# A four-bit quantization that starts two blocks earlier, and one more block in seven products

## The chip, the cores and the metric

The kernel runs on one core of a Trainium2 chip. A core has TensorE (PE, with the weight loads PEld), VectorE (DVE), ScalarE (ACT), GpSimd (POOL) and SyncE (SP), which here only issues transfers. Each engine works through its own queue in order, and semaphores make one wait for another. The metric is the device time of one execution in microseconds, the median of three runs. The profile is of one execution.

## The reference

128 matrices x of 64x512 are each multiplied by a 64x64 matrix that is picked from a table by an index. The result goes through two linear layers whose weights are made ternary (three values and a common factor), with an exact GELU between them. The output y of the second layer is quantized to four bits with one scale for the whole tensor, which comes from the largest |y|, and x is added.

```python
w = weights[conditions]
c = jnp.einsum('bct,bcd->bdt', x, w)
h = jax.nn.gelu(ternary_linear(c, W1, b1), approximate=False)   # 512 -> 2048
y = ternary_linear(h, W2, b2)                                   # 2048 -> 512
scale = jnp.max(jnp.abs(y)) / 7 + 1e-8
out = x + jnp.clip(jnp.round(y / scale), -7, 7) * scale
```

## The kernel before

The work goes through 16 blocks (`NB`), n = 0 to 15, of eight matrices each. A block has four pairs of matrices (`PAIRS`), 512 columns in all. Of each block the kernel first makes the mixed input (`condition` or `condition7`: `mix` on PE, then a high and a low part of the result by ACT and DVE), then goes through the 2048 hidden values in 16 steps of 128 (`hc` = 0 to 15), and adds each step's share of the second layer up in four accumulators (`py`). `result` turns these into y, `largest` takes the largest |y| of each row, and `keep` stores y to DRAM. The mixed input of block n + 1 is made during block n: `fetch` gathers the table's rows (POOL issues an indirect transfer into `wg`), `place` puts them into the matrix `diag`, and `mix` multiplies.

There are two ways through a block. `eight(s)` does one step: eight matmuls of 512 columns for the first layer (`ph`), and the second layer's matmuls two steps behind. `pair(n, k)` does two steps at once, k = 0 to 7, with `seven`: of the four products of a two-by-two split it computes seven smaller ones instead of eight, with sums of the weights (`sums`), in PSUM tiles x, y and z of 256 columns. ACT and DVE put the products together (`ha`, `hb`), ACT applies GELU and takes the high part, and DVE the low part (`low`). `behind(i)` is called at seven places of `seven` and issues what else belongs there: POOL's widened weights (`widen7`, `widen2`, into `wf`), the gather and placing of the next block, its mixing in pairs 3 to 6, the results of the block before in pairs 0 and 1, and its largest values in pairs 1 and 2. Blocks 2 to 13 go by `pair` (`SEVEN`), blocks 0, 1, 14 and 15 by `eight`.

The scale is speculative. `KNOWN` is 14: after block 13 the largest value of blocks 0 to 13 is found (`widened` reduces `ymax` to one column and copies it into all columns of `ones_f`, `largest_of` transposes this on PE and reduces again, `steps_of` makes `scale` and `inverse`). With it the output is made, while blocks 14 and 15 are still being computed, in 30 half blocks (`units`, in the order of blocks 2 to 13, 0, 1, 14): `quantize` on ACT, `add_x` on DVE one unit behind, `store` on SP, and `ahead_x`, which loads x two blocks ahead (`fetch_x`, and for blocks 0 and 1 also y from DRAM, `y_back`). `advance` does one such unit. The y of blocks 2 and up stays in SBUF until then, in the pool `big` of 20 buffers. At the end the largest value of the blocks left out is compared with the known one, and only if it is larger everything is quantized again under `tc.If`.

The queues are in program order on every engine (`InOrder`), so the place of a call in the text is its place in the queues of all the engines that it uses. Buffers come from pools, and who takes one waits until the readers of its former tile are through.

Of the kernel before, what the change touches and what calls it, by code (L numbers as in the profile page):

```python
# [8 lines left out]
F32 = mybir.dt.float32  # L9
# [11 lines left out]
P = 128  # L21
# [18 lines left out]
def tile_cond_ternary_ffn(  # L40
# [15 lines left out]
    B, C, T = x.shape  # L56
    S, _, D = weights.shape
    NT = T // P
    NH = W1.shape[1]
# [5 lines left out]
    GH = NH // NG  # L65
    WCH = GH * T
    LAG = 2
    SEVEN = range(2, 14)
    KNOWN = NB - 2
    AWAY = 2  # L70
    HALF = BLK // 2
    ADDED = [3, 4, 5, 6, 7, 12, 13, 14]
# [17 lines left out]
    def pair_of_pairs(h):  # L90
        return slice(h * PAIRS // 2, (h + 1) * PAIRS // 2)

    def load_x(n):

        xt = big.tile([P, PAIRS, T], F32, tag="big", name=f"xt_{n}")
        for h in range(2):
            js = pair_of_pairs(h)
            sp.dma_start(out=xt[:, js, :], in_=x_blk[n][:, js, :])
        return [xt[:, pair_of_pairs(h), :] for h in range(2)]

    def half_x(n, h):

        xt = half.tile([P, PAIRS // 2, T], F32, tag="half", name=f"xt_{n}_{h}")
        sp.dma_start(out=xt, in_=x_blk[n][:, pair_of_pairs(h), :])
        return xt

    def split_x(n):

        return [half_x(n, h) for h in range(2)]

# [792 lines left out]
    top_known = const.tile([P, 1], F32, name="top_known")  # L905
    scale = const.tile([P, 1], F32, name="scale")
    inverse = const.tile([P, 1], F32, name="inverse")
    order = [n for n in range(AWAY, KNOWN)] + list(range(AWAY)) + [NB - 2]
    units = [(n, h) for n in order for h in range(2)]
    xs, back, quantized, unstored = {}, {}, [], []  # L910

    def steps_of(scale, inverse, top):

        dve.tensor_scalar(scale, top, 1.0 / QMAX, EPS, ALU.mult, ALU.add)
        dve.reciprocal(inverse, scale)

    def keep(n):

        sp.dma_start(out=y_dram[n], in_=ys[n])

    def fetch_x(n):
        xs[n] = load_x(n)
        if n < AWAY:
            t = big.tile([P, PAIRS, T], F32, tag="big", name=f"y_back_{n}")
            sp.dma_start(out=t, in_=y_dram[n])
            back[n] = t
# [47 lines left out]
    def eight(s):  # L974

        n, hc = steps[s]
        if s + 1 < len(steps):
            ahead = steps[s + 1]
            if ahead[0] not in SEVEN:
                widen1(*ahead)  # L980
            else:
                widen7(0, 0)
        for c in {NH - 2: (NH - 3, NH - 2, NH - 1), NH - 1: ()}.get(
            hc if n == NB - 1 else None, [s + 1 - LAG - n * NH]
        ):
            widen2(*steps[n * NH + c])
        if s == len(steps) - 1:
            pool.drain()
        if n + 1 < NB:
            if hc == 0:  # L990
                if n + 1 == SEVEN[0]:
                    extra["x"] = half.tile([P, 2, T], F32, tag="half", name="x_quarters")
                    for j in range(2):
                        quarter_x(n + 1, j)
                else:
                    x_next.append(load_x(n + 1) if n + 1 < NB - 1 else split_x(n + 1))
                two_next.append(parts7(n + 1) if n + 1 in SEVEN else parts(n + 1))
            if 2 <= hc < 2 + PAIRS:
                fetch(n + 1, hc - 2)
            if 7 <= hc < 7 + PAIRS:  # L1000
                place(n + 1, hc - 7)
        if n == KNOWN and hc in (0, 1):
            fetch_x(order[hc])
        if n == SEVEN[0] - 1:
            for part in range(2):
                if hc - part in ADDED:
                    add_weights(ADDED.index(hc - part), part)
            if hc == NH - 2:
                widen7(0, 2)
                widen7(0, 3)  # L1010
        two = two_of(n, hc)

        ph = ps_h.tile([P, BLK], F32, tag="ph", name=f"ph_{n}_{hc}")
        layer1(n, hc, ph)

        bend(n, hc, ph, two, ph if n == NB - 1 else hf[hc % 2])
        hidden[n, hc] = two
        if s + 1 < len(steps) and steps[s + 1][0] in SEVEN and n not in SEVEN:
            widen7(0, 1)
        if n + 1 < NB and 8 <= hc < 8 + PAIRS:  # L1020
            j = hc - 8
            if n + 1 in SEVEN:
                for part in condition7(n + 1, j, extra["x"][:, j % 2, :], two_next[-1]):
                    part()
                if j + 2 < PAIRS:
                    quarter_x(n + 1, j + 2)
            else:
                condition(n + 1, j, pair_of(x_next[-1], j), two_next[-1])
            cond[n + 1] = two_next[-1]
        if hc == LAG:  # L1030
            for j in range(PAIRS):
                largest(n - 1, j)
            keep(n - 1)
        if n == KNOWN and hc == LAG:
            tops_known.append(widened(ymax[:, :KNOWN], "known"))
        if s == len(steps) - 1:
            low(n, hc)
            return
        if s == NH + 1:
            alpha_2()  # L1040
        behind = None if n == NB - 1 and hc in (11, 14) else s - LAG - (n == NB - 1 and hc > 11)
        if behind is not None:
            both_layer2(*steps[behind])
            if steps[behind][1] == NH - 1:
                for j in range(PAIRS):
                    result(n - 1, j)
        low(n, hc)
        if n == KNOWN and hc == LAG + 1:
            largest_of(tops_known.pop(), top_known, ps_c, "pc")
            steps_of(scale, inverse, top_known)  # L1050
        if n == KNOWN and hc > LAG + 1:
            advance(2 if hc in (6, 9, 12, 15) else 1)
        if n == NB - 1:
            advance(1)

# [2 lines left out]
    def widened(top, name):  # L1058

        top1 = const.tile([P, 1], F32, name=f"top1_{name}")  # L1060
        dve.tensor_reduce(top1, top.rearrange("p n j -> p (n j)"), AX.X, ALU.max)
        dve.tensor_copy(ones_f, top1.to_broadcast([P, P]))
        return ones_f

    def largest_of(wide, out, space, tag):
        tops = space.tile([P, P], F32, tag=tag, name=f"tops_{out.name}")
        pe.transpose(tops, wide, ident_f)
        dve.tensor_reduce(out, tops, AX.X, ALU.max)

    def pair(n, k):  # L1070

        s = n * NH + 2 * k
        ahead = (k + 1) % (NH // 2)
        leaves = ahead == 0 and n + 1 not in SEVEN
        before = steps[s - 2], steps[s - 1]

        def results(js):
            for j in js:
                result(n - 1, j)

        def behind(i):
            if i == 0:
                if k == 1:
                    results(range(1, PAIRS))
                widen2(*before[1])
                if k == 0:
                    two_next.append(parts7(n + 1) if n + 1 in SEVEN else parts(n + 1))
            if i == 1 and not leaves:
                widen7(ahead, 1)
            if i == 2:  # L1090
                if parting:
                    parting[0][0]()
                if leaves:
                    widen1(n + 1, 0)
                else:
                    widen7(ahead, 0)
            if i == 4:
                if not leaves:
                    widen7(ahead, 3)
                if k < PAIRS:  # L1100
                    fetch(n + 1, k)
                if 2 <= k < 2 + PAIRS:
                    place(n + 1, k - 2)
                if not leaves:
                    widen7(ahead, 2)
                if parting:
                    parting.pop()[1]()
                if k == 1:
                    quarter_x(n + 1, 0)
                    quarter_x(n + 1, 1)  # L1110
                if k in (4, 5):
                    quarter_x(n + 1, k - 2)
                if 3 <= k < 3 + PAIRS:
                    xp = extra["x"][:, (k - 3) % 2, :]
                    if n + 1 in SEVEN:
                        parting.append(condition7(n + 1, k - 3, xp, two_next[-1]))
                    else:
                        condition(n + 1, k - 3, xp, two_next[-1])
                    cond[n + 1] = two_next[-1]
            if i == 6:  # L1120
                widen2(*steps[s])
                if k == 0:
                    results([0])
                if k in (1, 2):
                    for j in (2 * k - 2, 2 * k - 1):
                        largest(n - 1, j)
                if k == 2:
                    keep(n - 1)

        seven(n, k, behind, before)  # L1130

# [122 lines left out]
```

## Time and profile before

| | us |
|---|---|
| median of 3 runs | 969.85 (969.79 to 970.12) |
| the profiled execution | 970.16 |
| its span, first to last instruction | 968.3 |
| PE busy | 957.5 |
| DVE / ACT / POOL busy | 660.6 / 613.5 / 656.5 |
| block 13, by pairs of seven products, on PE | 780.23 to 838.26 |
| block 14, by steps of eight products, on PE | 838.26 to 899.41 |
| first store of quantized output | 862.12 |
| transposition of the known maximum | 852.67 |

Rows of the timeline give the start, the duration, the engine, the operation, the tile written and the tiles read, and, in brackets, how long the engine had been idle before it and whose end it had waited for. A row with x2 or x8 holds several instructions in a run. The names of tiles have no numbers: `wf` is any widened weight tile, `ring` is also the home of `ha` and `hb`, `low_parts` is the low part of the hidden values. All instructions have one source line, that of the helper which records them. The chain is followed back from the last instruction, at each step to what released it.

### The profile page before, as it was taken

The numbers are of one execution on the slowest core, as the hardware profiler recorded it, in microseconds if no ns is written. First come the engines' busy times: TensorE is split into PE (matmuls) and PEld (weight loads), VectorE is DVE, ScalarE is ACT, GpSimd is POOL, SyncE is SP. The second block draws the span as 40 slices with busy tenths as digits, with TensorE's granted clock in tenths as the row PEclk, the third lists the DMA queues.
The fourth block names the chain that finished last, engine by engine and source line by source line (L and its number), as shares of the span: only waits on it lengthen the run. The fifth ranks groups of instructions, "written<-read, shape, count | busy, mean of one in ns | idle before, by whom it ended". The sixth has DMA issues, their size and how long they took to land.

```text
span 968.3 us, 16931 instructions
## 1 busy us (share of the span) xinstructions
PE 957.5 (99%) x5888; PEld 726.3 (75%) x5888; DVE 660.6 (68%) x1143; ACT 613.5 (63%) x1076; POOL 656.5 (68%) x1012
## 2 busy tenths in 40 slices
PE   8999999999999999999999999999999999999996
PEld 4687667877887887887878887887887878766664
DVE  7999766666666666666666666666667665467856
ACT  7995446666666566566666666566666666467773
POOL 5866867777676776767777676776767776566541
PEclk9999999999999999999999999999999999999999
DMA  9201011110111101011010111101011111339994
GB/s 358 100 23 47 14 34 50 33 58 17 32 49 33 59 24 65 19 34 50 34 58 17 33 48 33 60 24 67 16 34 50 33 59 47 109 133 374 392 406 179
DMA packets 33159, 80.06 MB, mean 83 GB/s; under 512 B 3760, under 2 KB 3760, under 8 KB 30128
## 3 DMA queue, kind: packets, MB, share of 16 engines
q1 hardware_dynamic: 31024, 76.86, 22.0%
q0 software_dynamic: 2048, 2.10, 0.7%
q8 instruction: 47, 0.77, 0.3%
q14 instruction: 40, 0.33, 0.1%
HBM read 46.44 MB, written 32.51 MB: 82 GB/s over the span
## 4 chain that ended last, share of the span: by engine, by line
PE 96%; DVE 2%; DMA 1%; ACT 0%; POOL 0%; issue 0%; SPq 0%; ACTq 0%
PE py L36 46%; PE xy L36 18%; PE z L36 14%; PE ph L36 12%; PE pc L36 6%; DMA nat<-in_L_ffn_W 1%; DVE top L36 1%; DVE xt L36 0%; DVE y_last L36 0%; ACT diag L36 0%; POOL wf L36 0%; PE number L36 0%; SPq L36 0%; ACT ph L36 0%; DVE terns L36 0%
## 5 line engine op out<-in xcount | busy, mean ns | idle before, releaser
L36 PE MATMUL py<-wf,h 128*128 128x512 f32 x1056 | 309.8, 418 | 0.0
L36 POOL CAST wf<-w2t 128x512 fp32r<-128x512 fp8e4 x234 | 201.4, 879 | 111.4 <-PE py L36 107.6
L36 DVE SCALAR_TENSOR_TENSOR low_parts<-ring,h 128x512 f16<-128x512 f32 x224 | 188.6, 876 | 85.6 <-ACT h L36 85.5
L36 PE MATMUL py<-w2t,low_parts 128*128 128x512 fp8e4 x944 | 228.0, 379 | 0.0
L36 PEld LDWEIGHTS py<-wf,h 128*128 128x128 f32 x1056 | 192.1, 189 | 44.8
L36 POOL CAST wf<-sums 128x256 fp32r<-128x256 fp8e4 (+1 forms) x288 | 142.6, 500 | 78.4 <-PE xy L36 75.2
L36 ACT ACTIVATE ring<-ring,b1t,alpha_up 128x512 f32<-128x512 f32 x192 | 156.0, 819 | 56.1 <-DVE ring L36 52.0
L36 DVE TENSOR_TENSOR ring<-xy,ring 128x256 f32<-128x256 f32 x192 | 106.5, 554 | 114.0 <-PE xy L36 114.0
L36 ACT COPY ring<-xy 128x256 f32<-128x256 f32 x192 | 71.4, 372 | 176.4 <-PE xy L36 176.4
L36 POOL CAST wf<-w1t 128x256 fp32r<-128x256 fp8e4 (+1 forms) x240 | 141.3, 600 | 27.8 <-PE ph L36 23.5
L36 PEld LDWEIGHTS <-low_parts 128*128 128x128 f16 x944 | 92.2, 98 | 88.8 <-issue 1.7
L36 ACT ACTIVATE h<-ring 128x512 fp32r<-128x512 f32 x224 | 130.2, 626 | 1.1
L36 POOL TENSOR_SCALAR diag<-wg 64x64 f32<-64x64 f32 (+1 forms) x116 | 65.9, 568 | 39.7 <-DMA wg<-in_L_cond_weights,rows 36.5
L36 PEld LDWEIGHTS <-w1t 128*128 128x128 fp8e4 x768 | 63.4, 98 | 32.7 <-issue 12.8
L36 PE MATMUL xy<-xb,wf 128*128 128x256 f32 x384 | 84.7, 302 | 0.0
L36 PE MATMUL xy<-xt,wf 128*128 128x256 f32 x384 | 75.4, 277 | 0.0
L36 PE MATMUL xy<-xl,sums 128*128 128x256 f16 x384 | 75.3, 278 | 0.0
L36 PE MATMUL xy<-xl,w1t 128*128 128x256 f16 x384 | 74.4, 275 | 0.0
L36 POOL DMA_INDIRECT wg<-in_L_cond_weights,rows x64 | 63.1, 986 | 16.5 <-issue 13.8
L36 PE MATMUL ph<-x,wf 128*128 128x512 f32 (+1 forms) x260 | 73.4, 404 | 0.3 <-POOL wf L36 0.3
L36 PE MATMUL z<-xl,sums 128*128 128x256 f16 x384 | 73.4, 273 | 0.0
L36 PEld LDWEIGHTS xy<-xt,wf 128*128 128x128 f32 x384 | 65.4, 188 | 8.6
(136 smaller groups left out, 1390.6 us busy)
## 6 DMA issues: line engine op xcount, KB each, us to landing
xt<-in_x SPq DMA_DIRECT2D x38, 512.0 KB, 7.1
y_dram<-y SPq DMA_DIRECT2D x15, 1024.0 KB, 4.0
out<-xt SPq DMA_DIRECT2D x30, 512.0 KB, 6.6
x_quarters<-in_x SPq DMA_DIRECT2D x52, 256.0 KB, 2.6
nat<-in_L_ffn_W SPq DMA_DIRECT2D x6, 1024.0 KB, 10.2
y_back<-y_dram SPq DMA_DIRECT2D x2, 1024.0 KB, 10.0
nat<-in_L_ffn_W SPq DMA_DIRECT2D x3, 512.0 KB, 8.9
wg<-in_L_cond_weights,rows POOLq DMA_INDIRECT x64, 2.4
```

The source lines that it names most:

```text
L36: return lambda *args, **kw: self._tc.keep_in_program_order(make(*args, **kw))
```

## The change

`KNOWN` becomes 12, and the range `SEVEN` takes in block 14. The maximum of blocks 0 to 11 is widened in pair 2 of block 12, and transposed in pair 3, in front of the product that uses `w12`. From pair 4 of block 12 on `advance(1)` stands at the front of every pair but pair 1, with a second one in pair 7, in blocks 12, 13 and 14; block 15 has one in each step as before. The loads of the first two x blocks move to pairs 0 and 1 of block 12. Block 15's x, for mixing, is loaded by quarters like that of the blocks before it, and the two functions that loaded it by halves go. The comparison at the end now takes in blocks 12 to 15.

```diff
-    SEVEN = range(2, 14)
-    KNOWN = NB - 2
+    SEVEN = range(2, NB - 1)
+    KNOWN = NB - 4
...
-    def half_x(n, h):
-
-        xt = half.tile([P, PAIRS // 2, T], F32, tag="half", name=f"xt_{n}_{h}")
-        sp.dma_start(out=xt, in_=x_blk[n][:, pair_of_pairs(h), :])
-        return xt
-
-    def split_x(n):
-
-        return [half_x(n, h) for h in range(2)]
...
-    order = [n for n in range(AWAY, KNOWN)] + list(range(AWAY)) + [NB - 2]
+    order = [*range(AWAY, NB - 2), *range(AWAY), NB - 2]
...
-                    x_next.append(load_x(n + 1) if n + 1 < NB - 1 else split_x(n + 1))
+                    x_next.append(load_x(n + 1))
...
-        if n == KNOWN and hc in (0, 1):
-            fetch_x(order[hc])
...
-        if n == KNOWN and hc == LAG:
-            tops_known.append(widened(ymax[:, :KNOWN], "known"))
...
-        if n == KNOWN and hc == LAG + 1:
-            largest_of(tops_known.pop(), top_known, ps_c, "pc")
-            steps_of(scale, inverse, top_known)
-        if n == KNOWN and hc > LAG + 1:
-            advance(2 if hc in (6, 9, 12, 15) else 1)
         if n == NB - 1:
             advance(1)
...
         def behind(i):
+            if i == 0 and n >= KNOWN:
+                if n == KNOWN and k < 2:
+                    fetch_x(order[k])
+                if k != 1 and (n > KNOWN or k > PAIRS - 1):
+                    advance(1)
+            if i == 2 and n >= KNOWN and k == NH // 2 - 1:
+                advance(1)
+            if i == 1 and n == KNOWN and k == PAIRS - 1:
+                largest_of(tops_known.pop(), top_known, ps_c, "pc")
+                steps_of(scale, inverse, top_known)
             if i == 0:
                 if k == 1:
                     results(range(1, PAIRS))
...
                 if k == 2:
                     keep(n - 1)
+                    if n == KNOWN:
+                        tops_known.append(widened(ymax[:, :KNOWN], "known"))
```

## The prediction

> **What bounds the kernel now.** I read the page first: busy times, then the chain that ended last.
>
> ```profile
> PE 957.5 (99%) x5888; PEld 726.3 (75%) x5888; DVE 660.6 (68%) x1143; ACT 613.5 (63%) x1076; POOL 656.5 (68%) x1012
> ...
> PE 96%; DVE 2%; DMA 1%; ACT 0%; POOL 0%; issue 0%; SPq 0%; ACTq 0%
> ```
>
> TensorE (PE) is busy for 99% of the span and carries 96% of the chain; the granted clock is 0.998. So only two things count: how much PE work there is, and where PE is made to wait. Next I read PE's timeline, where the first matmuls of blocks 13, 14 and 15 are:
>
> ```profile
> 780.23 0.40 PE L36 MATMUL xy<-xb,wf 128*128 128x256 f32 x2
> ...
> 838.26 1.09 PE L36 MATMUL ph<-x,wf 128*128 128x512 f32 x4
> ...
> 899.41 1.07 PE L36 MATMUL ph<-x,wf 128*128 128x512 f32 x4
> ```
>
> Block 13 (seven products) takes 838.26 - 780.23 = 58.03 us, block 14 (eight) 899.41 - 838.26 = 61.15 us. Inside a block of sevens, by the same timeline, pairs 0, 1, 2 and 7 take 6.81 us and pairs 3 to 6, which hold the mixing of the next block, 7.70 us, without a gap. The work that is moved must fit under these pairs, so I read ACT, DVE and POOL there. ACT between two plain pairs (0 and 1 of block 13):
>
> ```profile
> 785.58 1.14 ACT L36 ACTIVATE h<-ring 128x512 fp32r<-128x512 f32 x2
> 788.19 0.37 ACT L36 COPY ring<-xy 128x256 f32<-128x256 f32 x1 [1.48 <-PE xy L36]
> ```
>
> ACT idles 1.48 us there (1.60 after a mixing pair), waiting for PE. That copy ends 1.52 us into the pair, and PE rewrites its source at 1.85: 0.3 us to spare. DVE, around the old maximum and at the end:
>
> ```profile
> 743.02 1.27 DVE L36 TENSOR_REDUCE ymax<-y 128x1 f32<-128x512 f32 x2
> ...
> 850.69 0.21 DVE L36 TENSOR_REDUCE top_known<-ymax 128x1 f32<-128x56 f32 x1
> 850.94 0.43 DVE L36 COPY ones_f<-top_known 128x128 f32<-128x128 f32 x1
> ...
> 953.65 1.27 DVE L36 SCALAR_TENSOR_TENSOR xt<-y,scale,xt 128x1024 f32<-128x1024 int8 x1
> 954.85 0.74 DVE L36 SCALAR_TENSOR_TENSOR y_last<-py,alpha_up,b2b 128x512 f32<-128x512 f32 x1
> ```
>
> POOL, between pairs 3 and 4 of an earlier block and between pairs 2 and 3 of block 13:
>
> ```profile
> 402.81 0.37 POOL L36 TENSOR_SCALAR diag<-wg 64x64 f32<-64x64 f32 x1 [2.83 <-DMA wg<-in_L_cond_weights,rows]
> 403.24 0.61 POOL L36 CAST wf<-sums 128x512 fp32r<-128x512 fp8e4 x1
> ...
> 798.29 0.95 POOL L36 DMA_INDIRECT wg<-in_L_cond_weights,rows  x1 [0.28 <-issue]
> ...
> 800.79 0.56 POOL L36 TENSOR_SCALAR diag<-wg 64x64 f32<-64x64 f32 x1 [1.12 <-DMA wg<-in_L_cond_weights,rows]
> 801.42 0.61 POOL L36 CAST wf<-sums 128x512 fp32r<-128x512 fp8e4 x1
> ```
>
> and what the first of these did to the chain, where pairs of this kind otherwise stand 7.70 us apart:
>
> ```profile
> 399.05 3.11 PE py L36 x14
> ...
> 406.92 3.11 PE py L36 x14
> ```
>
> The reader should see that a weight gather (wg) that lands late holds POOL, that the widened weights (wf) behind it come late, and that PE lost 406.92 - 399.05 - 7.70 = 0.17 us.
>
> **The change, part by part.** The profiled execution is the ruler: 970.16 us, 968.3 of it span; the median of the runs, 969.85, lies 0.3 us below it. I apply the differences to the median.
>
> *Block 14 in sevens.* PE's 61.15 us become 58.03: **-3.12 us**. Its x comes by quarters into the buffer of the blocks before instead of two half tiles.
>
> *The end.* The order of units is the same, but 21 of 30 quantizations stand before block 15 instead of 16, so nothing of them is left near its end. Before, the add at 953.65 stood in front of y_last, which started at 954.85. PE's last matmul for that quarter (py<-w2t,low_last at 953.80, 0.39 us) ended at 954.19, so y_last can start at 954.22. From there DVE paces the end (its last y_last at 961.63, PE done at 960.67; 0.63 us earlier it is still DVE): **-0.63 us**.
>
> *The maximum.* The transposition now stands in pair 3 of block 12, on PE before the matmuls that stood at 744.01. DVE's reductions leave it free at 744.2; then the small reduction (0.25 to the next start) and the copy into ones_f: 0.43 us by the row above, 0.23 by the same copy at the kernel's end. ones_f is ready at 744.7 to 744.9, and weight load and matmul take 0.2. PE, and every matmul queued behind, goes on at 744.9 to 745.1 instead of 744.01. POOL is casting at that time, as in the 0.43 row, so I take the upper end: **+1.1 us**, ends 0.9 and 1.2. In block 14 the copy ended at 851.37 and the transposition ran at 852.67, so nothing waited.
>
> *One quantization (ACT) and one add (DVE) per pair.* 1.14 us on ACT go into the gap of 1.48 or 1.60 us: nothing, and beyond 0.3 to 0.5 us of lateness it is paid one for one. The add is 1.20 (alone) to 1.63 us (beside POOL's casts, in block 14); DVE's gap before the next pair's first sum is 1.1 to 1.2. That sum comes up to 0.4 us late, which a following idle of 0.50 takes up. Two places have less. Pair 7 gets two of each: the second add pushes the sums by up to 1.4 us, GELU and the next quantization follow, and the copy in the next pair 0 comes 0.1 to 0.45 us too late of which 0.3 is free. For the boundaries of blocks 12/13 and 13/14: 0 to 0.2 each, **+0.2 us** in all; 14/15 has no quantization behind it. Pair 2 has two reductions before the add; by the same walk pair 3's copy is 0.25 to 0.55 late, 0 to 0.3 lost, but the next item covers this.
>
> *Transfers past POOL's and SP's queues.* SP's stores and loads of block halves (512 KB each) begin in block 12. In pair 2 of blocks 13 and 14 the add ends about 3.9 us in; SP then issues at once a store of 512 KB, two loads of 512 KB, and the 1 MB store of y, which stood free before and now stands behind them. POOL's gather is issued at 4.44. It lands 2.3 to 2.5 us after its issue where nothing else moves; 3.4 to 3.9, twice 5.1 and 5.5, where a store of 1 MB started 0.9 us before; 5.3 to 6.3 at the kernel's start beneath the weight loads. The second placement waits for it, and the cast behind it ended at 802.03, 1.38 us into pair 3. The late case above gives the limit: its cast ended 1.86 us into the pair and cost 0.17, so 1.69 is free, and a landing up to 2.35 + 0.31 = 2.66 costs nothing. I take 3.4, the nearest row: a single transfer already moving. 0.74 us twice: **+1.5 us**; ends 0 (2.5) and 5.7 (5.5). Pair 3's gather comes later still, after the queue has run empty: 0. The quarter loads (issued at 755.58, landed in 2.6, needed by PE at 761.72) have 3.5 us to spare and lose about 2 to the add and the loads before them: 0. POOL's casts slow down beside the adds; those that PE needs have over 2 us, save the one above.
>
> [...]
>
> Sum: -3.12 - 0.63 + 1.1 + 0.2 + 1.5 = **-0.95 us**, so 969.85 - 0.95 = **968.9 us**.
>
> **Rivals.** *Faster by over 0.2% (1.94 us).* The gather lands within 2.9 us: 967.9 or less. With all of it hidden and the lower ends, -3.75 + 0.9 = -2.85: 967.0. For it: most gathers land in 2.4. Against: these had nothing moving beside them.
>
> *Slower.* The gather in pair 2 of blocks 13 and 14 waits behind all that SP has just issued. At 5.5 us: -3.75 + 1.1 + 0.2 + 5.7 = +3.25, 973.1; it decides from a landing of 4.85 us on. For it: 2.5 MB issued within 2 us, more than beside any gather after the start. Against: nine rows at 3.4 to 3.6 beside 1 MB.
>
> *The quantization is done twice.* If a maximum of blocks 12 to 15 were the larger, all 16 blocks would be loaded and stored again, 48 MB at the 390 GB/s of the page's busiest slices, over 120 us. Evaluating the reference gives 3.07 in block 1 and at most 2.83 in blocks 12 to 15, so this falls away.
>
> **How the numbers follow.** My sum 0.45 (967.9 to 971.5), the faster rival 0.25, the slower 0.23, something I don't see, mostly a wait more, 0.07. About 0.2% is what a measurement of this kernel can tell from no change. Faster: 0.23 of the rival, 0.04 of the sum's edge; slower: 0.20 and 0.06 of the unseen. The range takes the hidden case's end, 967.0, and most of the slow one: 973.0.
>
> **What the profile after would show.** Block 14 at 58 us plus waits; in PE's timeline a hole of about 1 us before the transposition at block 12, pair 3; holes of about 0.7 us in the same place of pair 3 in blocks 13 and 14, each under a POOL wait for wg of over 1.5 us (1.12 now); no add within 10 us of the end. If the holes in pair 3 exceed 2 us the slow rival holds; if there are holes in pairs 4 to 7, I have misjudged ACT's or DVE's cover, and that would make the prediction wrong with the mechanism elsewhere.

## The result, and the profile after

The changed kernel takes 976.18 us, the median of six runs (973.52 to 976.78), and the kernel before, beside it, 969.97 (969.79 to 970.17): a ratio of 1.0057, 95% interval 1.0043 to 1.0071, slower by 0.6%. The forecast was 968.9 us in a range of 967.0 to 973.0. The time lies above the range, on the side of the rival called slower. The profiled execution took 976.03 us, 974.2 of it span. The six times lie in two groups, 973.5 and 973.9 with a mean granted clock of 0.998, and 976.0 to 976.8 with 0.994 to 0.997; what may make the groups comes below.

The page of the changed kernel, PE's busy time and the chain, against 99% and 96% before:

```profile
PE 956.7 (98%) x5984; PEld 734.7 (75%) x5984; DVE 679.1 (70%) x1191; ACT 624.3 (64%) x1112; POOL 667.6 (69%) x1036
...
PE 94%; DVE 2%; DMA 2%; ACT 1%; POOL 0%; issue 0%; SPq 0%; POOLq 0%; DVEq 0%
```

PE's busy time fell from 957.5 to 956.7 us, while the span grew by 5.9 us: PE waits more. The view of waits lists what PE waited for (total, times, longest). The first and the fourth row are new; the other two were there before:

```profile
PE xy L36 <- POOL wf L36: 5.6, 2, 2.9
PE idle L36 <- POOL junk L36: 3.0, 1, 3.0
PE tops_top_rest L36 <- DVE ones_f L36: 2.9, 1, 2.9
PE tops_top_known L36 <- DVE ones_f L36: 1.2, 1, 1.2
```

PE's timeline gives their places, with the first matmuls of pairs 3 and 4 of block 13 and of blocks 14 and 15:

```profile
743.61 0.38 PE L36 MATMUL z<-xl,w1t 128*128 128x256 f16 x2
745.15 0.30 PE L36 MATMUL tops_top_known<-ident_f,ones_f 128*128 128x128 f32 x1 [1.17 <-DVE ones_f L36]
...
801.95 0.40 PE L36 MATMUL xy<-xb,wf 128*128 128x256 f32 x2
...
803.48 0.48 PE L36 MATMUL xy<-xb,wf 128*128 128x256 f32 x2
806.62 0.56 PE L36 MATMUL xy<-xt,wf 128*128 128x256 f32 x2 [2.66 <-POOL wf L36]
...
814.16 0.40 PE L36 MATMUL xy<-xb,wf 128*128 128x256 f32 x2
...
844.21 0.40 PE L36 MATMUL xy<-xb,wf 128*128 128x256 f32 x2
...
866.17 0.48 PE L36 MATMUL xy<-xb,wf 128*128 128x256 f32 x2
869.57 0.50 PE L36 MATMUL xy<-xt,wf 128*128 128x256 f32 x2 [2.92 <-POOL wf L36]
...
905.44 1.09 PE L36 MATMUL ph<-x,wf 128*128 128x512 f32 x4
```

The wait of 1.17 us is that of the transposition in pair 3 of block 12; the waits of 2.66 and 2.92 us lie in pair 3 of blocks 13 and 14, both for a widened weight tile. Such a time, in which PE has nothing that may start, is called a stand below. From the start of one pair to the next on PE, against 7.70 us for a pair with mixing, the stands cost more than they show as idle:

| place | length, us | lost, us | idle of PE, us |
|---|---|---|---|
| block 12, pair 3 | 9.18 | 1.48 | 1.17 |
| block 13, pair 3 | 12.21 | 4.51 | 2.66 |
| block 14, pair 3 | 10.90 | 3.20 | 2.92 |
| block 13, pair 5 | 7.86 | 0.16 | |

The last row is no stand in the view: the quarter load of that pair landed at 825.49, 6.1 us after its issue, and the mixing that reads it began at 825.63. Every other pair takes its 6.81 or 7.70 us. So the account from block 12 to the start of block 15 is: -3.12 for block 14 and +9.35 for four places, +6.23 us. The two profiled spans differ by 5.9 us, because the stretches ahead of block 12 and from block 15 on are 0.3 us shorter together; the medians differ by 6.21.

What POOL did in the second place, with SP's transfers of the same stretch in the second fence:

```profile
799.59 0.95 POOL L36 DMA_INDIRECT wg<-in_L_cond_weights,rows  x1 [0.26 <-issue]
800.56 0.41 POOL L36 TENSOR_SCALAR diag<-wg 64x64 f32<-64x64 f32 x1
805.52 0.37 POOL L36 TENSOR_SCALAR diag<-wg 64x64 f32<-64x64 f32 x1 [4.55 <-DMA wg<-in_L_cond_weights,rows]
805.95 0.61 POOL L36 CAST wf<-sums 128x512 fp32r<-128x512 fp8e4 x1
```

```profile
799.09 0.40 SPq L36 DMA_DIRECT2D out<-xt  x1
799.54 1.39 SPq L36 DMA_DIRECT2D xt<-in_x  x2
800.97 0.55 SPq L36 DMA_DIRECT2D y_dram<-y  x1
```

The gather issued at 799.59 landed 5.8 us later (6.0 in block 14). The first half of the placement ran at once; in front of the second half POOL stood 4.55 us, where it stood 1.12 before, and the cast that PE needs came behind it. Around the gather stand a store of 512 KB, two loads of 512 KB and a store of 1 MB. The packets of the DMA engines, too, show the gather held back: where nothing else moves, its first packet starts 1.7 us after the issue; here it started after 3.8 us, when 0.94 MB of SP's packets had started in between (3.9 us and 0.96 MB in block 14).

One stand is followed by something else. These are stretches of the span with PE's, PEld's, DVE's, ACT's and POOL's busy time, and then the granted clock, the DMA share and GB/s:

```profile
807.00:810.00 3.00, 3.00 (x15) 2.45 (x13) 0.42 (x1) 1.19 (x2) 2.10 (x6) 0.50 0.89 360
...
870.00:874.00 4.00, 4.00 (x30) 2.99 (x29) 1.81 (x3) 2.56 (x5) 3.63 (x8) 1.00 0.63 252
```

After the stand of 2.66 us in block 13 PE ran at half its clock, by single microseconds from 807 to 810 and at 0.83 in the next: some 3.3 us, which is about 1.7 us of work lost. After the 2.92 us in block 14 it did not. That is why 2.66 us of idle cost 4.51 and 2.92 only 3.20.

### The profile page after: what moved, and what is told of

Same layout as the page of the kernel before. It is cut to its first block, busy times and chain, and to the rows that moved or that the text cites. A ratio compares the mean times of both kernels' runs of the same rounds, so it can differ in the third digit from the quotient of the medians.

```text
span 974.2 us, 17245 instructions
## 1 busy us (share of the span) xinstructions
PE 956.7 (98%) x5984; PEld 734.7 (75%) x5984; DVE 679.1 (70%) x1191; ACT 624.3 (64%) x1112; POOL 667.6 (69%) x1036
## 4 chain that ended last, share of the span: by engine, by line
PE 94%; DVE 2%; DMA 2%; ACT 1%; POOL 0%; issue 0%; SPq 0%; POOLq 0%; DVEq 0%
PE py L36 45%; PE xy L36 20%; PE z L36 14%; PE ph L36 9%; PE pc L36 6%; DMA wg<-in_L_cond_weights,rows 1%; DMA nat<-in_L_ffn_W 1%; DVE top L36 1%; DVE xt L36 0%; POOL wf L36 0%; DVE y_last L36 0%; ACT diag L36 0%; DVE ymax L36 0%; PE number L36 0%; ACT ring L36 0%
## 5 line engine op out<-in xcount | busy, mean ns | idle before, releaser
L36 POOL CAST wf<-sums 128x256 fp32r<-128x256 fp8e4 (+1 forms) x312 | 163.9, 530 | 76.4 <-PE xy L36 72.9
L36 ACT ACTIVATE ring<-ring,b1t,alpha_up 128x512 f32<-128x512 f32 x208 | 168.5, 818 | 61.6 <-DVE ring L36 57.0
L36 DVE TENSOR_TENSOR ring<-xy,ring 128x256 f32<-128x256 f32 x208 | 115.1, 553 | 104.6 <-PE xy L36 104.3
L36 POOL CAST wf<-w1t 128x256 fp32r<-128x256 fp8e4 (+1 forms) x240 | 135.0, 575 | 27.3 <-PE ph L36 23.4
L36 PE MATMUL xy<-xb,wf 128*128 128x256 f32 x416 | 91.8, 302 | 0.0
L36 PE MATMUL xy<-xt,wf 128*128 128x256 f32 x416 | 82.2, 278 | 5.6 <-POOL wf L36 5.6
L36 PE MATMUL xy<-xl,sums 128*128 128x256 f16 x416 | 82.1, 279 | 0.0
L36 PE MATMUL z<-xl,sums 128*128 128x256 f16 x416 | 79.8, 273 | 0.0
L36 PEld LDWEIGHTS xy<-xb,wf 128*128 128x128 f32 x416 | 70.5, 190 | 9.5
L36 PEld LDWEIGHTS <-sums 128*128 128x128 fp8e4 x832 | 64.5, 98 | 13.5
```

The costliest lines, as they stand in the source:

```text
L36: return lambda *args, **kw: self._tc.keep_in_program_order(make(*args, **kw))
```

## The experiments

Two theories stood after the profile. By the first the loss is the gather alone, held up by the transfers around it; by the other POOL is short of time beside the adds and the gather is only the last in the row. The first four edits take the gather away from the transfers, take one or two of the transfers away from the gather, and move the transposition.

**The gather of pair 2 moved to pair 1** (blocks 13 and 14):

```diff
-                if k < PAIRS:
+                if n > KNOWN and k in (1, 2):
+                    if k == 1:
+                        fetch(n + 1, 1)
+                        fetch(n + 1, 2)
+                elif k < PAIRS:
                     fetch(n + 1, k)
```

> In blocks 13 and 14 the gather of pair 2 is issued in pair 1 beside that pair's own, where no store or load has just been started; all else is the changed kernel (976.2 us, profile 976.03). Theory: the whole loss of 4.51 and 3.20 us in pair 3 of blocks 13 and 14 is the wait for this gather and what follows from it. Then both pairs take 7.70 us, no matmul waits for wf, the granted clock stays at 1.00 there, and the kernel takes 976.03 - 7.71 = 968.3 us (968.0 to 968.8). Rival: POOL is short of time there beside the adds, and the gather is only the last in the row: pair 3 still loses over 1 us in each block, 970.5 us or more.

Measured: 971.63 us, 1.0016 [1.0006, 1.0025] of the kernel before. 4.5 us of the loss went, but not 7.7. Pair 3 of blocks 13 and 14 took 8.05 and 8.04, and pair 4 now 9.21 and 8.89. POOL in pair 3:

```profile
806.77 1.01 POOL L36 DMA_INDIRECT wg<-in_L_cond_weights,rows  x1 [0.16 <-issue]
807.81 0.39 POOL L36 TENSOR_SCALAR diag<-wg 64x64 f32<-64x64 f32 x1
811.23 1.43 POOL L36 TENSOR_SCALAR diag<-wg 64x64 f32<-64x64 f32 x1 [3.03 <-DMA wg<-in_L_cond_weights,rows]
```

The wait passed on to the next gather, issued 5.4 us after the 1 MB store had been (801.39) and landing after 4.3 us. Without the stall in pair 3, pair 3's gather came early enough to meet the same transfers, which kept the DMA engines busy until 810, and a new store of 512 KB, issued 0.4 us ahead of it. The 0.35 us that pair 3 still lost were not traced. The prediction had put that gather at nothing, "after the queue has run empty": it had done so only because POOL was late.

**The 1 MB store of y one pair later:**

```diff
-                if k == 2:
+                if k == (2 if n <= KNOWN else 3):
                     keep(n - 1)
+                if k == 2:
                     if n == KNOWN:
```

> The changed kernel with the 1 MB store of y of blocks 12 and 13 issued one pair later; before it, the store was issued 1.4 us after the gather. If the gather shares the engines with all that is queued, also what is issued after it, it lands after about 1.5/2.5 of 5.9 us, 3.6 us, and pair 3 loses about 0.9 us in each block: 976.2 - 5.9 = 970.3 us. If it waits only for what was issued ahead of it (a store of 512 KB and the two loads of 512 KB), the landing stays at 5.5 to 6.0 us and the time at 975.5 to 976.5 us.

Measured: 973.88 us (973.79 to 977.22), between the two; the gathers landed after 5.1 and 5.2 us, and pair 3 took 10.49 in both blocks. The time by itself says little: PE's stands are still 2.52 and 2.53 us, and some 1.6 us of the gain are the half clock, which this profile doesn't show. The landings say more. With the store 1.4 us behind the gather, in the changed kernel, the landings were 0.7 to 0.8 us later than here, and the first packet hardly so (3.8 and 3.9 us after the issue against 3.7 in both blocks); most of the delay is there with the 1.5 MB that start with the gather.

**The two loads of pair 2 one pair later** (`ahead_x` held back from `advance` in pair 2 and called in pair 3):

```diff
-                    advance(1)
+                    advance(1, held=late_x if n > KNOWN and k == 2 else None)
+                if k == 3:
+                    while late_x:
+                        ahead_x(late_x.pop())
```

> The changed kernel with the two loads of 512 KB that pair 2 of blocks 13 and 14 starts issued in pair 3; the store of 512 KB ahead of the gather and the store of 1 MB behind it stay. If all that is queued counts, 1.5 of 2.5 MB are left, and the gather lands after 3.6 us: about 0.9 us lost in each block, 970.3 us. If only what is ahead of it counts, 0.5 MB is left, and it lands after 2.5 to 3.4 us: 0 to 0.7 us lost in each, 968.5 to 969.9 us.

Measured: 976.48 us (974.91 to 977.04), nothing gained; landings of 5.2 and 5.9 us. Both numbers expected were wrong, and the trace says why: with the loads gone, SP issued the 1 MB store of y at 799.78 instead of 800.97, right before the gather's 799.82. The edit moved one transfer away and the next one up. With 1.5 MB just ahead of it or beside it, whichever, the gather took 5.1 to 5.9 us in these two runs. Here all 1.5 MB had been issued ahead of it, and the gather's first packet started when 1.57 and 1.56 MB of SP's had, after 4.4 us.

**The transposition two steps later:**

```diff
-            if i == 1 and n == KNOWN and k == PAIRS - 1:
+            if i == 3 and n == KNOWN and k == PAIRS - 1:
```

> The changed kernel with the transposition for the maximum placed two steps further back in the same pair, 1.4 us of matmuls later. Theory: PE stood 1.17 us because ones_f comes at 745.0 and the matmul was due at 743.97; behind 1.4 us of matmuls it is ready in time, pair 3 of block 12 takes 7.7 to 7.9 instead of 9.18 us, and the kernel takes 1.2 to 1.5 us less than the changed one: 974.7 us. Rival: the wait moves on, because the mixing's products use the same PSUM buffers as the transposition and wait for DVE to read them, or because the scale comes too late for the quantization of pair 4: gain under 0.5 us.

Measured: 974.45 us (973.04 to 974.56), pair 3 of block 12 in 7.83 us, no wait for `ones_f`: as expected.

The next edit takes all four gathers out of the way.

**Gathers two by two in pairs 0 and 1:**

```diff
-                if k < PAIRS:
+                if n > KNOWN:
+                    if k < 2:
+                        fetch(n + 1, 2 * k)
+                        fetch(n + 1, 2 * k + 1)
+                elif k < PAIRS:
                     fetch(n + 1, k)
```

> The changed kernel with the four gathers of blocks 13 and 14 issued two in pair 0 and two in pair 1, so that none is issued near the 2.5 MB that start in pair 2. With one gather moved, the wait had passed on to the next one. Theory: with no gather left behind those transfers there is no wait to pass on: pairs 3 and 4 of both blocks take 7.70 us, and of the profile's 976.03 us the 4.51 and 3.20 go: 968.3 us (968.0 to 968.8). Rival: the placements of pairs 3 to 5 are late for POOL's own lack of time beside the adds; then pairs 3 and 4 keep over 0.5 us each, 969.5 us or more.

Measured: 976.16 us, no better than the changed kernel, though POOL never waits for wg in blocks 13 and 14. Pairs 1 and 2 of both blocks now take 8.69 and 8.54 instead of 6.81. DVE in pair 1 of block 13, then POOL beside it:

```profile
787.76 4.22 DVE L36 SCALAR_TENSOR_TENSOR low_parts<-ring,h 128x512 f16<-128x512 f32 x2 [1.40 <-ACT h L36]
```

```profile
787.54 0.94 POOL L36 DMA_INDIRECT wg<-in_L_cond_weights,rows  x1 [0.30 <-issue]
788.48 0.63 POOL L36 CAST wf<-sums 128x512 fp32r<-128x512 fp8e4 x1
789.03 1.17 POOL L36 CAST wf<-w2t 128x512 fp32r<-128x512 fp8e4 x2
790.14 0.40 POOL L36 CAST wf<-sums 128x256 fp32r<-128x256 fp8e4 x1
790.49 0.95 POOL L36 CAST wf<-w1t 128x256 fp32r<-128x256 fp8e4 x2
```

The second gather holds POOL 1.3 us longer, and its casts then run without a gap from 788.48 to 791.44, nearly all at their short durations. DVE's two low parts, 1.71 us together in the changed kernel, end only at 791.98: the first took 0.69 us, the second, from 788.37 on, 3.61. There the casts were the slow ones, the pair on `w2t` taking 1.99 us instead of 1.17. PE then stands 1.66 us for ACT's copy of z, which waits for the low parts. In pair 2 it stands 0.79 us for a widened weight tile and 0.56 for ACT, so there POOL, with a second gather in front of its casts, comes late as well.

So either side is found held up in these runs, where the prediction had counted on slower casts on POOL and on up to 0.43 us (1.63 less 1.20) for DVE's add. In the kernel before it was a cast: on `w1t`, 0.62 us long at 858.55, it took 1.39 at 861.18, beside an add of 1.63 us. Here it is the low part: its 3.61 us run beside six casts and not beside one, although its own row begins 0.11 us before the first of them. What decides which side is held up, no run shows.

**That, with the transposition later:** the diff is the one above.

> The same with the transposition for the maximum two steps later too. If the two causes are independent their gains add: 968.3 less 1.35 us (9.18 to 7.83 in pair 3 of block 12) = 967.0 us, which is the -3.12 us of block 14 and no other wait. If the one hides behind the other, 968 us or more.

Measured: 974.98 us, 1.18 less than without. The step is worth about the same here; the 967.0 stood on a base of 968.3 that had not come.

**That, with the last add earlier:** `hc > 9` sets `final`, so that the last unit's add comes in step 10 of block 15.

```diff
         if n == NB - 1:
-            advance(1)
+            advance(1, hc > 9)
```

> The same, and the add of the last unit is made at the sixth step from the end of block 15, not after its loop. Theory: the last y_last starts 0.63 us earlier because no add of 1.28 us stands before it on VectorE, 967.0 - 0.6 = 966.4 us. Rival: the end is set by something else (the other y_last, TensorE), 967.0 us.

Measured: 974.25 us, 0.73 less again. In the traces the first `y_last` now starts 1.18 us after the last low part does, instead of 1.80.

**What a stand of PE costs.** The kernel before with a transposition in pair 7 of blocks 3 to 11 that waits for a chain on DVE:

```diff
+        def stand(copies):
+            for _ in range(copies):
+                dve.tensor_scalar(ones_f, ones_f, 1.0, None, ALU.mult)
+            tops = ps_c.tile([P, P], F32, tag="pc", name=f"tops_stand_{n}")
+            pe.transpose(tops, ones_f, ident_f)
+            dve.tensor_reduce(top_known, tops, AX.X, ALU.max)
...
+            if i == 1 and k == 7 and n in STAND:
+                stand(STAND[n])
```

> The kernel before, with a transposition in pair 7 of blocks 3 to 11 that waits for 8, 12, 16, 20, 8, 12, 16, 20 and 30 chained copies of 128 x 128 on VectorE; the output stays what it was. Theory: a longer stand of TensorE is at times followed by some 3.4 us at half the clock, as after the 2.66 us in block 13 (4.51 us lost), so that stands from 2.5 us on cost up to 1.7 us more than their length, in some places and not in others, and short ones their length. Rival: the lost 1.85 us in block 13 belong to something else, for example the traffic there; then each stand costs its length, and the clock stays at 1.00.

Measured: 1025.0 us (1023.95 and 1026.05). Pair by pair, against 6.81 us:

| idle of PE, us | lost in the pair, us | beyond the idle, us |
|---|---|---|
| 2.13 (blocks 3, 7) | 2.43, 2.42 | 0.3, 0.3 |
| 3.18 (blocks 4, 8) | 6.10, 4.93 | 2.9, 1.8 |
| 4.22 (blocks 5, 9) | 6.99, 6.11 | 2.8, 1.9 |
| 5.27 (blocks 6, 10) | 7.48, 7.15 | 2.2, 1.9 |
| 7.89 (block 11) | 9.99 | 2.1 |

The stand of 3.18 us in block 4, in slices of two microseconds after the transposition at 316.36, shows 0.50, 0.50 and 0.51; after the stands of 2.13 us no slice is below 0.99. All seven stands of 3.18 us or more are followed by half a clock, neither of the two of 2.13 is. Over stretches of 12, 10, 10 and 8 us around the stands of blocks 4, 5, 6 and 8 the mean granted clock is 0.72, 0.66, 0.66 and 0.79. This run has no transfers of the change beside the stands, so the traffic is not needed for it, and the rival falls away. What is lost beyond the idle, 1.8 to 2.9 us, is more than the 1.7 expected. Between 2.13 and 3.18 us the length alone does not decide: of the eight stands of 2.5 to 2.9 us for wf in the profiles of the changed kernel and of the three in which the gather of pair 2 stayed where it was, three were followed by it (2.66, 2.52 and 2.81 us) and five not (2.52, 2.53, 2.65, 2.78, 2.92). All three lie in block 13, of four there, and none of the four in block 14 had it; whether that is chance was not tested.

The next edit uses what the rows of the changed kernel show: the placement that waits in pair 2 puts the gather of pair 0 into place, and needs nothing of the one just issued. If POOL waits for that one only because it is issued ahead, the other order takes the wait away.

**Place first, gather after,** in every pair:

```diff
-                if k < PAIRS:
-                    fetch(n + 1, k)
                 if 2 <= k < 2 + PAIRS:
                     place(n + 1, k - 2)
+                if k < PAIRS:
+                    fetch(n + 1, k)
```

> The changed kernel with one order turned round: in each pair POOL places the weights of two pairs ago first and issues its gather after that, so that a placement never stands behind the gather just issued. The gathers stay one per pair and as late as they were. Theory: the placement needs nothing of the late gather; POOL only waits for it because it was issued before; so the landing may stay at 5 to 6 us and yet pairs 3 and 4 of blocks 13 and 14 take 7.70 us: of 976.03 us, 4.51 and 3.20 go, 968.3 us (968.0 to 968.8). Rival: the wait passes on to the next pair's placement, as it did with one gather moved (1.5 and 1.2 us in pair 4): 970.5 us or more; or VectorE is locked out by POOL's casts as with the gathers in pairs 0 and 1: 971 us or more.

Measured: 969.93 us, 0.9998 [0.9988, 1.0008] of the kernel before, 6.25 less than the changed kernel. Pair 3 takes 7.75 and 7.77 us. In the POOL timeline of block 13 the gather stands behind the placement, and no placement waits:

```profile
799.45 0.81 POOL L36 TENSOR_SCALAR diag<-wg 64x64 f32<-64x64 f32 x2
800.53 1.01 POOL L36 DMA_INDIRECT wg<-in_L_cond_weights,rows  x1 [0.27 <-POOL diag L36]
```

That gather lands after 6.5 us (6.7 in block 14), later than in the changed kernel, and it costs nothing. So the transfers delay the gather, and the order on POOL makes the delay a loss. Why in the old order only the second half of the placement was held, the record does not show. The time is still 1.6 us over the 968.3 expected: block 13 loses 0.59 us in pair 4 and 0.48 in pair 5, block 14 0.39 in pair 4. ACT, then DVE, in pairs 3 and 4 of block 13:

```profile
808.53 0.83 ACT L36 ACTIVATE ring<-ring,b1t,alpha_up 128x512 f32<-128x512 f32 x1
809.25 1.15 ACT L36 ACTIVATE h<-ring 128x512 fp32r<-128x512 f32 x2
810.29 1.15 ACT L36 ACTIVATE y<-y,inverse 128x1024 int8<-128x1024 f32 x1
811.33 0.37 ACT L36 COPY ring<-xy 128x256 f32<-128x256 f32 x1
812.13 0.58 ACT L36 COPY ring<-z 128x512 f32<-128x512 f32 x1 [0.42 <-DVE low_parts L36]
```

```profile
801.99 1.76 DVE L36 SCALAR_TENSOR_TENSOR low_parts<-ring,h 128x512 f16<-128x512 f32 x2 [1.51 <-ACT h L36]
803.68 1.26 DVE L36 TENSOR_REDUCE ymax<-y 128x1 f32<-128x512 f32 x2
804.86 1.69 DVE L36 SCALAR_TENSOR_TENSOR xt<-y,scale,xt 128x1024 f32<-128x1024 int8 x1
806.47 0.41 DVE L36 TENSOR_TENSOR ring<-xy,ring 128x256 f32<-128x256 f32 x1
...
810.14 1.90 DVE L36 SCALAR_TENSOR_TENSOR low_parts<-ring,h 128x512 f16<-128x512 f32 x2
```

and PE, in pairs 4 and 5:

```profile
812.76 0.38 PE L36 MATMUL z<-xl,sums 128*128 128x256 f16 x2 [0.21 <-ACT ring L36]
...
822.25 1.13 PE L36 MATMUL pc<-diag,x_quarters 128*128 128x128 f32 x8 [0.25 <-DMA x_quarters<-in_x]
```

With the stall gone, DVE goes from the low parts through two reductions and the add to the sums without a gap; GELU, quantization and copy follow late on ACT, and the copy of z that PE waits for stands 0.42 us for DVE's next low parts. In the changed kernel the stall had hidden this: DVE and ACT caught up while PE stood. The quarter load had not been hidden. It was issued 2.4 us before pair 5 there as here; there its lateness cost the 0.16 us of the table above, here 0.48. The same order in the kernel before, where there are no such transfers:

> The kernel before with the same order turned round. There no transfer over 1 MB stands near a gather, and its one late case cost 0.17 us: 969.9 to 970.1 us, no difference, if the order matters only under the new transfers. Rival: it is worth something by itself, 969.5 us or less, and then a part of what place_first gains isn't the change's.

Measured: 970.05 us against 970.10, 1.0000 [0.9990, 1.0009]: no difference, so the whole gain is of the change's own loss.

**With the transposition later,** and then **the last add earlier too:**

> That, with the transposition for the maximum two steps later: 968.3 less 1.35 = 967.0 us (966.7 to 967.5), 0.3% below the kernel before. Rival: 968 us or more, if one wait had hidden the other.

> That, with the last unit's add made six steps before the end of block 15: 967.0 - 0.7 = 966.3 us, as the same edit took 0.73 us (974.98 to 974.25) from the kernel with the gathers in pairs 0 and 1. Rival: 967.0 us, if that was chance.

Measured: 968.86 us, 0.9985 [0.9976, 0.9995], and 967.95 us (967.51 to 968.44), 0.9977 [0.9967, 0.9986] of the kernel before. The steps took 1.07 and 0.91 us. The first took 1.37 us off pair 3 of block 12, but pair 5 of block 13 became 0.26 longer. Both times are over the numbers expected, and over the rivals' too, by what is left in pairs 4 and 5 (1.7 and 1.6 us). The last one is the fastest version found; it beats both kernels.

## Why the prediction was wrong

*Block 14 in sevens: right.* Its eight pairs take 61.23 us (844.21 to 905.44), without the 3.20 us lost by the stand 58.03, and -3.12 us is there.

*The end: the step "nothing of them is left near its end" failed.* VectorE in the changed kernel has the same three rows as before, six microseconds later:

```profile
959.10 0.69 DVE L36 SCALAR_TENSOR_TENSOR low_last<-ph,high_last 128x512 f16<-128x512 f32 x1 [1.05 <-ACT high_last L36]
959.71 1.28 DVE L36 SCALAR_TENSOR_TENSOR xt<-y,scale,xt 128x1024 f32<-128x1024 int8 x1
960.90 0.75 DVE L36 SCALAR_TENSOR_TENSOR y_last<-py,alpha_up,b2b 128x512 f32<-128x512 f32 x1
```

The add runs one unit behind the quantization, so however early the 30th quantization is, the 30th add waits for the loop after block 15, `advance(1, True)`. The worth of the add was right: with the add moved, `y_last` starts 0.62 us sooner in the traces, where 0.63 had been worked out, and the medians fell by 0.73 and 0.91 us. The change just doesn't move it. The sign given for it, no add within 10 us of the end, could not tell: this add stood over 14 us before the end with and without the change.

*The maximum: mechanism right, size a little short.* PE waited 1.17 us in the predicted place, inside the bounds of 0.9 to 1.2. The pair lost 1.48, over the upper end: 0.31 us more than the idle, as with the two stands of 2.13 us, which cost 2.43 and 2.42. That 0.3 is missing in the sum.

*One quantization and one add per pair.* The +0.2 us at the pairs 7 did not come: these pairs kept 6.81 us. In the changed kernel no pair 4 lost anything, but that was cover lent by the stall. Without it, 0.59 and 0.39 us are lost in pair 4, which had been costed at nothing. The quarter load, with "3.5 us to spare", is late once: it landed 6.1 us after its issue, where 2.6 had been assumed, which cost 0.16 us in pair 5 of block 13, and 0.48 with the placement first.

*Transfers past the queues: the mechanism was seen, the value chosen was wrong.* This term was put at +1.5 us and measured 7.71, and with it the forecast falls: the rival "slower" held, decided from a landing of 4.85 us on, and the landings were 5.8 and 6.0. Its sign, holes of over 2 us in pair 3, is there with 2.66 and 2.92. Its arithmetic holds. By the free 2.66 us these landings should cost 3.1 and 3.3 us; the idle of PE, 2.66 and 2.92, with the 0.3 behind each, is 3.0 and 3.2. Two things were off. The first is the choice of 3.4 us, "the nearest row": those nine rows had 1 MB beside them, here 1.5 MB started within a microsecond of the gather and 1 MB more behind it. With 2.5 MB, the upper end was the nearer one. And what the gather met was more than "a single transfer already moving": in six landings of 5.1 to 6.0 us, in the changed kernel and the two with transfers moved, 0.93 to 1.57 MB of SP's packets started before the gather's first. In a row of 3.4 us, at 791.49 of the kernel before, 0.98 MB of the 1 MB store's packets had. The second is the clock: about 1.6 us of the 4.51 in block 13 are half-speed matmuls after the stand (4.51 less 2.66 less 0.3), a term that was not in the sum at all. Without it the kernel would be at about 974.5, still above the range.

The size of the landing is measured, not explained. That the gather of 128 rows waited for most of what SP had issued ahead of it is shown by the landings, 2.3 to 2.6 us alone and 5.1 to 6.7 in these stretches, and by its first packet, which started after 1.7 us alone and after 3.7 to 5.4 here. Why it does was not settled.

## What to carry to other kernels

A small transfer that is issued beside large ones should be priced by the bytes that are issued ahead of it and around it (here a gather landed after 2.3 to 2.6 us alone and after 5.1 to 6.7 with 1.5 to 2.5 MB there), and the order of an in-order queue should never put a wait for it ahead of work that does not need it: here turning two calls round gave back all 6 us, while moving the transfer moved the wait. When a stall goes, price what it had been covering, and when a step is said to be gone from the end, follow the counter that emits it to its last call. A stand of TensorE can cost more than its length: here 1.7 to 1.9 us more in three of eight stands of 2.5 to 2.9 us and 1.8 to 2.9 in all seven of 3.18 to 7.89, about 0.3 in the others.

## What the runs showed of the hardware

The granted clock fell to 0.50 after some stands of PE, for about 3.3 us in the changed kernel and for over 5 us after the stand of 3.18 us in block 4. It did so after every one of seven stands of 3.18 to 7.89 us, after three of eight of 2.5 to 2.9 us, and after neither of two of 2.13 us. Stands of 2.52, 2.66 and 2.81 us were enough for it, and others of 2.52 to 2.92 us were not; what decides between them, no run shows. The half clock explains the two groups of the changed kernel's times in part at most: the mean clock of the faster group is 0.998, as in the kernel before, but the groups lie some 2.5 us apart, one such stretch costs 1.7, and no execution of the faster group was profiled.

VectorE lost against GpSimd here as well as the other way round: in the changed kernel two low parts take 1.71 us together and the two casts on `w2t` beside them 1.99; with a second gather ahead on POOL the low parts took 4.22 while POOL's six casts ran back to back (788.48 to 791.44), the two on `w2t` in 1.17. The 1.3 us of delay on POOL were enough to turn it.
